# Wide column copies in the opening of a fused network, and a line-innermost spectrum with inner statistics in its third layer

## Chip, cores and metric

One NeuronCore of a Trainium2 chip runs the whole network in one launch, in float32. The metric is the device time of one execution in microseconds (us); lower is better. Engines are named as in the profile: PE (TensorE matmuls), PEld (TensorE's loads of stationary weights, which overlap PE), DVE (VectorE), ACT (ScalarE), POOL (GpSimd), SP (SyncE, which issues all DMAs here). SBUF and PSUM are the two on-chip memories, of 128 partitions each; matmuls write PSUM.

## The reference

Four images of 64x64 pixels with 128 channels pass four layers. Each adds to its input: `x = x + layer(group_norm(x))`.

- Layer 0 is a selective scan. A projection makes 256 channels and 256 gates per pixel; the channels go through a 3x3 depthwise convolution and a SiLU. The result is scanned along four paths: by rows, by columns, and both backwards. Per path a projection gives step sizes `delta`, `B` and `C`, and with 16 states a channel `h = exp(delta*A)*h + delta*u*B` runs over all 4096 pixels, `y = h*C`. The sum is normed, multiplied by SiLU of the gates, projected.
- Layer 1 multiplies low Fourier modes along each axis and applies two dense layers.
- Layer 2, the third, treats each of the 128 channels of an image as a token, a 64x64 picture ("CoDANO"). Instance norm `in(.)` is over the pixels of one token:

```python
tn   = in1(tokens)
k, q, v = (spectral_conv(tn, w) + skip for w in (key, query, value))   # 16 heads; k, q at 32x32
attn = softmax(q k^T / scale) v
attn = in_a(spectral_conv(attn, proj_w) + skip + tokens)               # spectral_conv: rfft2, low modes x w, irfft2
m    = in2(attn)
m    = gelu(in_m1(spectral_conv(m, mixer_w1)) + skip1(m))
m    = in_m2(spectral_conv(m, mixer_w2)) + skip2(m)
out  = in_o(m) + attn
```

- Layer 3 is attention in 7x7 neighbourhoods.

## The kernel before

**Layer 0.** An image is `[channels, pixels]`, in two halves `s` of 128 channels and eight chunks `c` of 512 pixels (eight rows of the image). The scan takes, for 128 units (image, path, chunk) of 16 states each, POOL's product `dB` (L651), ACT's `dA` (L656) and DVE's scan (L657); `units[0]` is chunk 0 by rows, unit 8 the first by columns. Everything else of this layer runs beside the scans from a table of slots, except for the **opening** (`opening`, from L190), which must come before the first scan and has its own written order.

The opening reads image 0, norms it (L215 to L217), and then for `c` = 0 to 5 (`DENSE = 6`): `scale` norms the chunk and projects half 1 (L224 to L227); `padded` copies half 0's chunk with its border (POOL, L234); `depthwise` convolves half 1 on DVE, nine operations (L241, L248); `conv` convolves half 0 on PE in nine passes (L164); `gates` makes the two gates. `silu` is three ACT passes and a product on DVE, with a DMA of the result: `e = exp(-v)`, `ln(1+e)`, `exp(-e)` (L198 to L200), `e = v*e` (L343). `grown` ends a convolved half with its `silu` and with `by_columns` (L351 to L355): ACT copies the chunk into a tile `xw` with columns outermost, and an SP DMA writes it to DRAM array `xw0`, where a column's 64 pixels lie together; a chunk has eight rows, so each run is 8 floats, 32 B. The gates of chunks 6 and 7 follow. `e`, `xw` and other tiles share four buffers (tag `t2`). Into the list `steps` are woven the inputs of unit 0: after chunk 1 `fetch` (u), after chunk 3 `begun` (projection `xd_ps`, copies `xc` and `cc`, and `Bb`, the broadcast of B from DRAM, of three buffers), after chunk 4 `readied` (`d`, `e`, `l`, `m` of both halves: projection `dp`, exp, log, limit; then `du` on POOL). For these and `dp` a bank of PSUM comes from `spare` (one bank, tag `m`).

**Layer 2.** `layer2_image` (L1070 on) is a generator that issues one image's instructions and yields at each wait. `Pace.in_turn` advances two images at a time, always the one whose modelled time is least; `Pace.spend` keeps the modelled time of engines (all of the layer's instructions are recorded at its line, L1043, in the profile). The order that it finds is fixed at build time. The stages are: load and group norm; `token_stats` of the input (`bn_stats` of 32 blocks of 128x128, then three small products `in_pm`); `dft_y`, a transform along lines (PE, to PSUM `pu`, ACT copies it to `U`); `px`, the second transform (PE loads a slice of `U` as weights); `pv`, `pG`, a Gram matrix for the attention scores; scores, softmax `S`; `pk` for the skips; `pz`, the attention-weighted product for both images of the pair (weights `WX`); `synthesis` (PE `pa`, ACT copy to `S2`, PE `pb`; its `put` adds `pb` to `z`); the statistics of `z`, from which the norm's scale `sa` and shift `za`; then twice `spectral` (`dft_y`, `pq` times `mix`, `synthesis`, whose `put` copies to `sp`), with statistics of `sp` behind each; mixing with `m` and gelu behind the first; and the tail behind the second: `sp` scaled and added to `m`, statistics of `m`, `x` loaded again into `sp`, and `z*sa + f3 + m*q3 + x` to the output. `by_rows` is one DVE operation on 128x1024 with a scale for each token; `affine` is eight ACT operations on 128x128. Images 0 and 1 run together, then 2 and 3.

In `U`, of shape `[P, 64, 2, 32]`, the transformed axis is innermost, so the slice for one frequency, over 64 lines, steps by 64 floats:

```python
nc.tensor.matmul(px[:, e, :], lhsT=U[:, :, q, 4 * g + e], rhs=w["quad"][:, q, :], ...)
```

and in `V`, `[66, 64, 8]`, the slice `V[:, :, e]` steps by 8 floats.

Of the kernel before, what the change touches and what calls it, by code (L numbers as in the profile page):

```python
# [84 lines left out]
def layer0(sh, A, x_in, x_out, scr):  # L85
# [7 lines left out]
    with ExitStack() as ctx:  # L93
# [79 lines left out]
        def grown(b, c, s, pm, later, e=None):  # L173
            bias = conv_b[:, s : s + 1], conv_nb[:, s : s + 1]
            xo = silu(pm, *bias, scr(f"xr{b % 2}")[s, :, c * CH : (c + 1) * CH], later, (0, 1, 2), e)
            later("act0", by_columns, xo, scr(f"xw{b % 2}")[s], c, slots=4)

        def gates(b, c, v, bank, later):
            for s in range(2):
# [3 lines left out]
                silu(zp, 0.0, 0.0, scr(f"z{b % 3}")[s, :, c * CH : (c + 1) * CH], later, (0, 0, 1))  # L183
# [6 lines left out]
        def opening(bank, steps):  # L190
# [3 lines left out]
            def soon(place, f, *a, slots=1, **kw):  # L194
                if place == "dve" or f is by_columns:
                    waiting[place[:3]].append(lambda: f(*a, **kw))
                else:
                    f(*a, **kw)  # L198

            now = lambda place, f, *a, slots=1, **kw: f(*a, **kw)  # L200
            pair = lambda name: tmp.tile([P, 2, CH], F32, name=name, tag="t4", bufs=4)
# [52 lines left out]
            for c in range(DENSE + 1):  # L254
# [6 lines left out]
                if last:  # L261
                    grown(0, c - 1, 0, last[0], soon, pair("e")[:, 0])
                    grown(0, c - 1, 1, last[1][:, 0], soon, last[1][:, 1])
# [14 lines left out]
            for c in range(DENSE, NCH):  # L278
                for _ in gates(0, c, xg[:, 8 * c : 8 * c + 8], bank, now):
# [135 lines left out]
        def inputs(k, c, u, par):  # L415
# [64 lines left out]
        def fetched():  # L480
            u, v = fetch(*units[0])
            do, ready, bd, Wd = inputs(*units[0][1:], v, 0)
# [6 lines left out]

        def readied():  # L490
            for name in ("d0", "e0", "l0", "m0", "d1", "e1", "l1", "m1", "du"):
# [119 lines left out]
        with tc.manual_schedule(engines=order):  # L611
            idle = lambda: None
            left = opening(any_bank, [idle, fetched, idle, begun, readied])
            u, ready, bd, Wd, Bb = (got[n] for n in ("u", "ready", "bd", "Wd", "Bb"))
            sides.append(Side(rest(left, spare, later), 18 * len(left), 0, 2 * NS * len(left)))
            for i, (b, k, c) in enumerate(units):
# [22 lines left out]
                for n in range(NS):  # L639
# [34 lines left out]
                    if i + 1 < len(units):  # L674
                        if n == 1:
                            u_next, v_next = fetch(*units[i + 1])
                            do, ready_next, bd_next, Wd_next = inputs(*units[i + 1][1:], v_next, (i + 1) % 2)
# [335 lines left out]
class Pace:  # L1013


    def __init__(self, nc):
        self.nc, self.free, self.t, self.first = nc, {}, 0.0, None

    def spend(self, name, op, out):
# [11 lines left out]
        self.free[name] = end  # L1031
        self.first = self.first or name
# [45 lines left out]
def layer2_image(sh, w, pools, x_in, x_out, scr, wt, parity, beside):  # L1078
# [16 lines left out]
    def token_stats(src):  # L1095


        st = own([P, NJ, 6], "in_st")
        for j in range(NJ):
            nc.vector.bn_stats(st[:, j, :], src[:, j, :])  # L1100
            if j % 8 == 7:
                yield j == NJ - 1
# [44 lines left out]
    def dft_y(src):  # L1147

        U = large("U2", [P, 64, 2, 32])
        for g in range(NJ // 4):  # L1150
# [3 lines left out]
            nc.scalar.copy(U[:, 8 * g : 8 * g + 8].rearrange("p t q r -> p (t q r)"), pu.rearrange("p q m -> p (q m)"))  # L1154
# [3 lines left out]
    def synthesis(Z, put):  # L1158
# [20 lines left out]
        for g0 in range(0, 16, 4):  # L1179
# [13 lines left out]
            yield g0 == 12  # L1193

# [68 lines left out]
    for g in range(8):  # L1263
        px = ps.tile([64, 4, Q], F32, name="px", tag="b")
        for e in range(4):
            for q in range(2):
                nc.tensor.matmul(
                    px[:, e, :], lhsT=U[:, :, q, 4 * g + e], rhs=w["quad"][:, q, :], start=(q == 0), stop=(q == 1)
# [25 lines left out]
    for v, r0, r1 in ((1, 0, 8), (2, 8, 9), (0, 9, 16), (3, 16, 17), (0, 17, 24), (1, 24, 32), (None, 0, 0)):  # L1294
        nr = r1 - r0
        if nr:
            V = tmp.tile([66, 64, 8], F32, name="V2", tag="S2", bufs=3)
            pv = ps.tile([66, 64, nr], F32, name="pv", tag="a")
            for q in range(2):
                nc.tensor.matmul(pv, lhsT=w["gram"][:, v, q, :], rhs=U[:, :, q, r0:r1], start=(q == 0), stop=(q == 1))  # L1300
            nc.scalar.copy(V[:, :, :nr], pv)
        if V_last is not None:
            for e in range(V_last[1]):
                Ve = V_last[0][:, :, e]
# [135 lines left out]
    yield from synthesis(Zp, lambda u, g0, p: tt(at(z, u, g0), at(z, u, g0), p, ALU.add))  # L1440
# [3 lines left out]
    mu, var = yield from token_stats(z)  # L1444
# [17 lines left out]
    def spectral(src, mix):  # L1462
        U = yield from dft_y(src)
        Zm = own([Q, 64, 32], "Zp", tmp)
        for g in range(4):
            px = ps.tile([Q, 16, 32], F32, name="pq", tag="b")
            for q in range(2):
                nc.tensor.matmul(
                    px, lhsT=w["quad"][:, q, :], rhs=U[:, 16 * g : 16 * g + 16, q, :], start=(q == 0), stop=(q == 1)
                )  # L1470
            tt(Zm[:, 16 * g : 16 * g + 16, :], px, mix.unsqueeze(1).to_broadcast([Q, 16, 32]), ALU.mult)
# [532 lines left out]
```

## Time and profile before

| quantity | value |
|---|---|
| time before, median of 3 runs | 7942.88 us (7941.58 to 7944.81) |
| the profiled execution's own time | 7939.57 us |
| its span, first to last instruction | 7937.7 us |
| mean granted TensorE clock | 0.959 |

Stretches of the profiled execution, busy us of each engine:

| stretch (us from the span's start) | length | PE | DVE | ACT | POOL |
|---|---|---|---|---|---|
| opening, to the first scan: 0 to 153.2 | 153.2 | 86.9 | 85.8 | 78.6 | 19.3 |
| scans of layer 0: to 5790 | 5636.8 | 4595.8 | 5388.4 | 5189.6 | 5175.6 |
| layer 1: to 6319 | 529.0 | 454.5 | 298.0 | 150.8 | 0.0 |
| layer 2: to 7366 | 1047.0 | 760.9 | 565.0 | 340.3 | 102.0 |
| layer 3: to 7937 | 571.0 | 493.8 | 430.8 | 386.0 | 191.3 |

In the lines that follow, a group of instructions reads: line, engine, operation, output and input by the program's names, shapes, count | busy us, mean ns of one | idle time of the engine just before them and what ended it. A line of a timeline reads: start, duration, engine, line, operation, and in brackets the wait before it with what ended it. A line of the chain of waits reads: start, length, engine, tile, line, number of instructions. A line by stretches reads: the stretch, its length, then PE, PEld, DVE, ACT and POOL busy with counts, granted clock, DMA share and GB/s.

### The profile page before, as it was taken

The numbers are of one execution on the slowest core, as the hardware profiler recorded it, in microseconds if no ns is written. First come the engines' busy times: TensorE is split into PE (matmuls) and PEld (weight loads), VectorE is DVE, ScalarE is ACT, GpSimd is POOL, SyncE is SP. The second block draws the span as 40 slices with busy tenths as digits, with TensorE's granted clock in tenths as the row PEclk, the third lists the DMA queues.
The fourth block names the chain that finished last, engine by engine and source line by source line (L and its number), as shares of the span: only waits on it lengthen the run. The fifth ranks groups of instructions, "written<-read, shape, count | busy, mean of one in ns | idle before, by whom it ended". The sixth has DMA issues, their size and how long they took to land. (4 is left out here: it accounts for less than half of the span.)

```text
span 7937.7 us, 140991 instructions
## 1 busy us (share of the span) xinstructions
PE 6391.9 (81%) x52796; PEld 4053.1 (51%) x52796; DVE 6768.0 (85%) x8012; ACT 6145.3 (77%) x9814; POOL 5488.2 (69%) x2510
## 2 busy tenths in 40 slices
PE   6888888878888877888987777787778888686789
PEld 2544444444455444445554444454457665464566
DVE  6999999999999999999999999999845645645678
ACT  5999999999999999999999999999822223315567
POOL 2989999988999998999999999999800010020233
PEclk8999999999999999999999999999989988788899
DMA  9556556545556554555555445555442230331332
GB/s 149 161 169 176 176 173 176 168 165 167 188 172 185 179 169 165 172 183 177 177 187 169 167 162 182 175 172 188 149 111 46 55 106 21 91 106 39 99 95 80
DMA packets 1392574, 1159.91 MB, mean 146 GB/s; under 512 B 759829, under 2 KB 1186417, under 8 KB 1324946
## 3 DMA queue, kind: packets, MB, share of 16 engines
q1 hardware_dynamic: 1390210, 1149.16, 47.9%
q8 instruction: 416, 6.82, 0.4%
q14 instruction: 268, 2.20, 0.1%
q10 hardware_dynamic: 1680, 1.74, 0.1%
HBM read 956.89 MB, written 189.74 MB: 144 GB/s over the span
## 5 line engine op out<-in xcount | busy, mean ns | idle before, releaser
L657 DVE TENSOR_TENSOR_SCAN h<-dA,state,dB 128x512 f32<-128x512 f32 x4096 | 4920.2, 1266 | 191.6 <-ACT dA L656 71.3
L651 POOL TENSOR_TENSOR dB<-du,Bb 128x1024 f32<-128x1024 f32 x2048 | 4812.5, 2388 | 358.8 <-DVE h L657 237.6
L511 PE MATMUL pt<-ident,h 128*128 128x128 f32 x16384 | 2219.5, 279 | 872.2 <-ACT hT L521 861.2
L656 ACT ACTIVATE dA<-delta,A_neg 128x512 f32<-128x512 f32 x4096 | 2760.5, 697 | 151.7 <-DVE h L657 123.8
L511 PEld LDWEIGHTS pt<-ident,h 128*128 128x128 f32 x16384 | 1809.5, 141 | 1923.0 <-ACT hT L521 1706.2
L521 ACT COPY hT<-pt 128x1024 f32<-128x1024 f32 x2048 | 2079.6, 1015 | 164.0 <-PE pt L511 144.9
L546 PE MATMUL yT<-hT,W 128*32 128x256 f32 x16384 | 1378.0, 409 | 1.0 <-ACT hT L521 0.6
L1043 POOL COPY XG<-Xs 64x9 f32<-64x9 f32 (+2 forms) x44 | 10.9, 292 | 960.5 <-ACT Xs L1043 960.5
L546 PEld LDWEIGHTS yT<-hT,W 128*32 128x32 f32 x16384 | 454.9, 150 | 339.9 <-issue 327.4
L164 PE MATMUL cv<-xn,taps 128*128 128x512 f32 x936 | 526.9, 644 | 2.8 <-DVE delta L451 2.8
L1724 POOL TENSOR_TENSOR S<-S,sm 128x784 f32<-128x784 f32 x128 | 191.3, 1494 | 436.4 <-DVE sm L1722 366.7
L454 POOL TENSOR_TENSOR du<-delta,u 128x1024 f32<-128x1024 f32 x128 | 304.7, 2381 | 96.9 <-DVE delta L451 96.9
L442 PE MATMUL dp<-xd,w_dt 65*128 65x512 f32 x512 | 289.9, 648 | 68.8 <-ACT Ct L433 41.3
L425 PE MATMUL xd_ps<-u,w_x 128*48 128x512 f32 x512 | 248.9, 609 | 44.9 <-DVE e L343 39.4
L1731 ACT ACTIVATE S<-S,mx 128x196 f32<-128x196 f32 x512 | 227.9, 448 | 35.2 <-DVE mx L1758 34.6
L164 PEld LDWEIGHTS cv<-xn,taps 128*128 128x128 f32 x936 | 139.2, 188 | 180.7 <-issue 160.6
L851 ACT ACTIVATE h<-pf,b 128x512 f32<-128x512 f32 x128 | 88.0, 687 | 145.0 <-PE pf L850 145.0
L451 DVE SCALAR_TENSOR_TENSOR delta<-delta,dp 128x512 f32<-128x512 f32 x256 | 170.7, 667 | 13.9 <-ACT delta L448 10.7
L1686 PE MATMUL pt<-ident,S 128*98 128x128 f32 x1024 | 167.0, 288 | 3.6 <-POOL S L1724 1.9
L448 ACT ACTIVATE delta<-delta 128x512 f32<-128x512 f32 x256 | 165.9, 648 | 0.1
L442 PEld LDWEIGHTS dp<-xd,w_dt 65*128 65x128 f32 x512 | 76.6, 188 | 173.9 <-ACT Ct L433 94.4
L445 ACT ACTIVATE delta<-dp 128x512 f32<-128x512 f32 x256 | 153.0, 598 | 9.8 <-PE dp L442 8.4
(366 smaller groups left out, 6934.2 us busy)
## 6 DMA issues: line engine op xcount, KB each, us to landing
Bb<-l_B SPq DMA_DIRECT2D x512, 1024.0 KB
W<-l_W SPq DMA_DIRECT2D x512, 256.0 KB
l_y<-y SPq DMA_DIRECT2D x128, 512.0 KB
u<-l_xr SPq DMA_DIRECT2D x64, 512.0 KB
u<-l_xw SPq DMA_DIRECT2D x64, 512.0 KB
y<-l_y SPq DMA_DIRECT2D x56, 512.0 KB
V<-l_v SPq DMA_DIRECT2D x512, 49.0 KB
y<-l_y SPq DMA_DIRECT2D x80, 256.0 KB
```

The costliest lines, as they stand in the source:

```text
L164: nc.tensor.matmul(pm, lhsT=taps[:, s, t, :], rhs=xn[:, dy : dy + 8, dx : dx + 64], start=(t == 0), stop=(t == 8),)
L425: nc.tensor.matmul(bank["x"], lhsT=w_x[:, s, k, :], rhs=u[:, s, :], start=(s == 0), stop=(s == 1))
L442: nc.tensor.matmul(bank[s], lhsT=w_dt[:, k, s * P : (s + 1) * P], rhs=xd, start=True, stop=True)
L454: nc.gpsimd.tensor_tensor(du, delta, u, ALU.mult)
L511: nc.tensor.transpose(pt[:, j, s, :], G["h"][:, s, t0 : t0 + 32, :].rearrange("p t n -> p (t n)"), sh.ident)
L521: return lambda: nc.scalar.copy(hT, pt.rearrange("p j s d -> p j (s d)"))
L546: nc.tensor.matmul(U["yT"][e][32 * jo : 32 * jo + 32, qo % 2, :], lhsT=U["Ws"][G["g"]][:, :, 4 * q + j], rhs=hT[:, j, :], start=((e, jo) n ...
L651: nc.gpsimd.tensor_tensor(dB, du, B_now[:, q : q + 1, :].to_broadcast([P, 2, CH]), ALU.mult)
L656: nc.scalar.activation(dA, delta[:, s, :], AF.Exp, scale=A_neg[:, k, s, n : n + 1])
L657: nc.vector.tensor_tensor_scan(h[:, s, :, q], dA, dB[:, s, :], state[:, s, n : n + 1], ALU.mult, ALU.add)
L1724: nc.gpsimd.tensor_tensor(Sv, Sv, U["sm"].unsqueeze(2).to_broadcast([P, 4, 196]), ALU.mult)
L1731: nc.scalar.activation(Sn, Sn, AF.Exp, bias=U["mx"][:, n : n + 1], accum_out=sm[:, n : n + 1])
```

## The change

Opening:

- `gather` takes the place of `by_columns`. ACT copies each chunk into a wide tile for four chunks (`[P, 4, 512]`, from the three buffers of `Bb`), columns outermost, so that a column of the tile has 32 rows; one DMA for each half writes chunks 0 to 3 after chunk 3's copy (runs of 128 B, 1 MB), and one for each half chunks 4 and 5 after chunk 5's (runs of 64 B, 512 KB).
- The gates of chunks 6 and 7 get buffers of their own (`pair("e")`, tag `t4`).
- `readied` is split: `d`, `e`, `l` of both halves in chunk 4's turn, `m` and `du` in chunk 5's; their order is d0, d1, e0, e1, l0, l1. The opening takes their banks from `any_bank`, four in turn.

Layer 2:

- `U` becomes `[P, 2, 32, 64]`, `V` `[66, 8, 64]`, `pq` `[Q, 32, 16]`: lines innermost. The weights of `px` and both operands of `pG` are then read without a step. ACT's copy into `U` reads PSUM with a step of 64 floats and DVE's product of `pq` reads it with a step of 16 floats.
- The statistics of `z` and of both `sp` are taken inside `synthesis`, four blocks behind each `put` (`counted`). `Pace` charges them to DVE without advancing the image's own time (`aside`).
- `residual`: POOL replaces `z` by `z*sa + za + x` in place, three operations on 128x1024 for each of four quarters, issued during the first `spectral`; `x` is loaded there, into a buffer of its own, `xr`.
- `grown`: POOL scales `m` by the second skip's weight during the second `spectral` (four operations on 128x1024).
- Tail: 32 DVE operations on 128x128 make `m = sp*q2 + m`, each eight followed by their statistics. Then, for three quarters, `affine` on ACT (`m*q3 + f3`) and one addition of `z` on DVE; for the last, eight DVE operations `m*q3 + z` and one `by_rows` with `f3`.

```diff
-            later("act0", by_columns, xo, scr(f"xw{b % 2}")[s], c, slots=4)
+            later("act0", gather or by_columns, xo, scr(f"xw{b % 2}")[s], c, slots=4)
...
+            def gather(xo, s, c):
+                n = 4 if c < 4 else DENSE - 4
+                first = c % 4 == 0
+                if first:
+                    wide[s] = tmp.tile([P, 4, CH], F32, name="xw", tag="Bb", bufs=3).rearrange("p q t -> p (q t)")
+                t = wide[s][:, : 512 * n].rearrange("p (w h) -> p h w", w=64)
+                h0 = 8 * (c % 4)
+                nc.scalar.copy(t[:, h0 : h0 + 8], xo.rearrange("p (h w) -> p h w", w=64))
+                if c % 4 == n - 1:
+                    nc.sync.dma_start(
+                        scr("xw0")[s].rearrange("p (w h) -> p w h", h=64)[:, :, 8 * c - 8 * n + 8 : 8 * c + 8],
+                        t.rearrange("p h w -> p w h"),
+                    )
...
-                for _ in gates(0, c, xg[:, 8 * c : 8 * c + 8], bank, now):
+                es = pair("e")
+                for _ in gates(0, c, xg[:, 8 * c : 8 * c + 8], bank, now, (es[:, 0], es[:, 1])):
...
+        def grown_steps():
+            for name in ("d0", "d1", "e0", "e1", "l0", "l1"):
+                got["do"][name]()
+
         def readied():
-            for name in ("d0", "e0", "l0", "m0", "d1", "e1", "l1", "m1", "du"):
+            for name in ("m0", "m1", "du"):
                 got["do"][name]()
...
-            left = opening(any_bank, [idle, fetched, idle, begun, readied])
+            left = opening(any_bank, [idle, fetched, idle, begun, grown_steps, readied])
...
+    def counted(st, src, js):
+        nc.aside = True
+        for j in js:
             nc.vector.bn_stats(st[:, j, :], src[:, j, :])
+        nc.aside = False
...
-        U = large("U2", [P, 64, 2, 32])
+        U = large("U2", [P, 2, 32, 64])
...
-            nc.scalar.copy(U[:, 8 * g : 8 * g + 8].rearrange("p t q r -> p (t q r)"), pu.rearrange("p q m -> p (q m)"))
+            nc.scalar.copy(
+                U.rearrange("p q r t -> p (q r) t")[:, :, 8 * g : 8 * g + 8],
+                pu.rearrange("p j m -> p (j m)").rearrange("p (t k) -> p k t", t=8),
+            )
...
-                    px[:, e, :], lhsT=U[:, :, q, 4 * g + e], rhs=w["quad"][:, q, :], start=(q == 0), stop=(q == 1)
+                    px[:, e, :], lhsT=U[:, q, 4 * g + e, :], rhs=w["quad"][:, q, :], start=(q == 0), stop=(q == 1)
...
-                Ve = V_last[0][:, :, e]
+                Ve = V_last[0][:, e, :]
                 nc.tensor.matmul(pG, lhsT=Ve, rhs=Ve, start=(n_done == 0), stop=(n_done == 31))
...
-    yield from synthesis(Zp, lambda u, g0, p: tt(at(z, u, g0), at(z, u, g0), p, ALU.add))
+    st = own([P, NJ, 6], "in_st")
+
+    def added(u, g0, p):
+        tt(at(z, u, g0), at(z, u, g0), p, ALU.add)
+        counted(st, z, block(u, g0))
+
+    yield from synthesis(Zp, added)
...
+        def copied(u, g0, p):
+            nc.scalar.copy(at(sp, u, g0), p)
+            counted(st, sp, block(u, g0))
+            nc.aside = True
+            next(beside, None)
+            nc.aside = False
...
+    def residual():
+        xr = large("xr")
+        load_image(nc, xr, x_in)
+        for n, c in enumerate(C4):
+            wide = lambda v: v[:, c].unsqueeze(2).to_broadcast([P, 8, DM])
+            for v, op in ((wide(sa), ALU.mult), (wide(za), ALU.add), (xr[:, c, :], ALU.add)):
+                nc.gpsimd.tensor_tensor(z[:, c, :], z[:, c, :], v, op)
+            if n % 2:
+                yield
...
+    def grown():
+        for n, c in enumerate(C4):
+            nc.gpsimd.tensor_scalar(m[:, c, :], m[:, c, :], scal(10), None, ALU.mult)
+            yield
...
-        if n % 2:
-            by_rows(sp, sp, q2, n, ALU.mult)
-        else:
-            affine(sp, sp, q2, None, n)
-        stt(m[:, c, :], m[:, c, :], scal(10), sp[:, c, :], ALU.mult, ALU.add)
-        nc.sync.dma_start(sp[:, c, :], x_in[1024 * n : 1024 * n + 1024, :].rearrange("(j p) d -> p j d", p=P))
+        js = range(8 * n, 8 * n + 8)
+        for j in js:
+            stt(m[:, j, :], sp[:, j, :], q2[:, j : j + 1], m[:, j, :], ALU.mult, ALU.add)
+        counted(st, m, js)
...
-        affine(z, z, sa, f3, n)
-        by_rows(m, m, q3, n, ALU.mult)
-        tt(m[:, c, :], m[:, c, :], sp[:, c, :], ALU.add)
-        yield False
-        tt(m[:, c, :], m[:, c, :], z[:, c, :], ALU.add)
+        if n == 3:
+            for j in range(8 * n, 8 * n + 8):
+                stt(m[:, j, :], m[:, j, :], q3[:, j : j + 1], z[:, j, :], ALU.mult, ALU.add)
+            by_rows(m, m, f3, n, ALU.add)
+        else:
+            affine(m, m, q3, f3, n)
+            yield False
+            tt(m[:, c, :], m[:, c, :], z[:, c, :], ALU.add)
```

## The prediction

> **What bounds the kernel now.** I read the page first, then the timeline of the opening by queue, the groups by shape in the third layer's stretch, its chain of waits and its busy time by stretch. The page says that no engine bounds the whole:
>
> ```profile
> PE 6391.9 (81%) x52796; PEld 4053.1 (51%) x52796; DVE 6768.0 (85%) x8012; ACT 6145.3 (77%) x9814; POOL 5488.2 (69%) x2510
> ```
>
> DVE's 85% is the first layer's scan (4920.2 us), which the change leaves alone. It touches two stretches: 0 to 153.2 us, before the first scan, and the third layer, from its first load at 6319 to 7366. In the opening, ACT's timeline shows who holds the first scan back:
>
> ```profile
> 131.65 0.60 ACT L200 ACTIVATE e<-zp 128x512 f32<-128x512 f32 x1 [4.39 <-DMA l_xw<-xw]
> 137.31 0.60 ACT L200 ACTIVATE e<-zp 128x512 f32<-128x512 f32 x1 [3.74 <-DMA l_xw<-xw]
> 143.96 0.60 ACT L200 ACTIVATE e<-zp 128x512 f32<-128x512 f32 x1 [4.74 <-DMA l_xw<-xw]
> 150.60 0.60 ACT L200 ACTIVATE e<-zp 128x512 f32<-128x512 f32 x1 [4.72 <-DMA l_xw<-xw]
> 153.20 20.22 DVE L657 TENSOR_TENSOR_SCAN h<-dA,state,dB 128x512 f32<-128x512 f32 x17
> ```
>
> Gates 6.3 us apart, each waiting for the tile of a column copy: a 256 KB column copy of 8192 runs of 32 B costs the DMA engines 6.3 us, and twelve of them stand in this stretch.
>
> In the third layer the weight loads of two groups stand out, beside one that reads its weights without a step:
>
> ```profile
> L1043 PEld LDWEIGHTS pz<-PT,WX 128*68 128x68 f32 x2048 | 131.8, 146 | 20.0 <-DVE WX L1043 17.1 <-POOL WX L1043 1.7 <-issue 1.1
> L1043 PEld LDWEIGHTS px<-quad,U 128*64 128x64 f32 x512 | 57.8, 204 | 2.1 <-ACT U L1043 1.7
> L1043 PEld LDWEIGHTS pG<-V 66*64 66x64 f32 x256 | 32.5, 216 | 10.7 <-issue 10.3 <-ACT V L1043 0.3
> ```
>
> Busy by count: pz 64 ns a pass, px 113, pG 127. The chain has them at 112.7 (px x96 in 10.82), 126 (pG x30 in 3.79), 62.4 (pz x544 in 33.94).
>
> Then its back half, where the chain goes through statistics while PE stands:
>
> ```profile
> 7118.65 6.40 PE pb L1043 x24
> ...
> 7125.77 10.84 DVE in_st L1043 x56
> ...
> 7136.66 5.33 PE in_pm L1043 x24
> ...
> 7335.29 6.20 DVE in_st L1043 x32
> ```
>
> ```profile
> 7320.00:7370.00 50.00, 2.95 (x12) 2.71 (x12) 35.00 (x62) 21.33 (x60) 0.00 (x0) 0.50 0.42 122
> ```
>
> In the last 50 us PE works 2.95, DVE 35, ACT 21, POOL nothing: elementwise work.
>
> **Opening.** Twelve column copies become four: two of 8192 runs of 128 B (1 MB), two of 8192 runs of 64 B. Undisturbed, a chunk takes 10.44 us (L227's copies at 40.58 and 51.02: ACT's silus 8, DVE's product and scale 1.2, PE's pv 1.1). So L227 of chunk 3 comes at 61.5 instead of 65.7; chunk 4 at 74.1 (PE: conv to 70.9, xd_ps 1.9, pv 0.9); chunk 5 at 87.1 (two dp, two exp, two ln, which now run side by side). The column copies of chunk 4 follow at 95.1. They take a buffer from the three of "Bb", and the first two wide DMAs must have left it: issued at 84.5. Their price: by the descriptor count 6.3 us each, by bytes (256 KB in 6.3) 25 us each. I take 8: the count is unchanged, the runs are longer. They land at 92.5 and 100.5, so ACT stands 4.5 us. Then silus of chunk 5 (3.9), two copies (1.9), four gates on own buffers (4x1.81): first scan at 115.5. Queued behind SP's two 64 B transfers are now the second and third Bb, which wait for that landing: Bb lands near 125, where the fifth row of scans wants its product; I charge 3. Gain 153.2-115.5-3 = 35 (28 to 42). A column copy into a step of 128 B has no row; the one with a step of 32 B takes 1.13 us, one without a step 0.59; I keep 1.13 (0.6 to 2.2, twelve of them, a chunk's worth hidden by PE's 10.3 us). The gates' own buffers and the three banks for the first dp and xd_ps have no instruction; their worth is in the sum.
>
> **Front of the third layer.** px's weights and both operands of pG lose their step. px mirrors pz then (64 columns loaded, 68 streamed): 64 ns. 512x(113-64) = 25, 256x(126-64) = 16, together 41. Up to 7100 the chain holds 7.2% + 3.9% of 784 us, 87 of their 95.5 busy: 37 us gained. Both ends: 0, if the loads are slow for another reason, and 41.
>
> Here a rule stands against the change. ACT now copies U out of PSUM with a step of 256 B, and DVE multiplies pq with a step of 64 B:
>
> ```profile
> L1043 ACT COPY Zp<-pz 68x512 f32<-68x512 f32 x16 | 9.3, 582 | 140.9 <-PE pz L1043 140.9
> ```
>
> This copy already reads with that very step and takes 582 ns, the plain U copy 585. The Trainium skill ("SBUF — State Buffer", Door 1: The DMA port swizzle, its note on cachelines) gives PSUM lines of 8 B and SBUF lines of 16 B and a penalty for each access that leaves its line. For SBUF weights row and rule agree. For PSUM the row denies it on ACT: 96 U copies cost nothing more; doubled they would add 0.55 at each of 12 tails, 7 us. For DVE no row reads PSUM with a step: 0.69 as now, or 1.02 as TENSOR_REDUCE Pb with a step beside 0.69 for mx; PE's 1.72 per pq hides all but eight tails, 0 to 3 us, I take 1, inside the rounding.
>
> **Back half, by pairs of images.** Statistics of z are taken block by block beside PE's 1.9 us per pair of pb: of 10.84 us 0.8 remains, -10. Statistics of sp likewise; the second image's (4x1.55) leave the first's mixing, so the second mixes 14 us sooner. What is added: per image twelve POOL operations on z (128x1024), put from the first step of the first synthesis on. By dB (2.38 us) 24 take 57 us a pair, by Z<-TT,W alone 1.90. Whom they meet:
>
> ```profile
> 6458.51 1.90 POOL L1043 TENSOR_TENSOR Z<-TT,W 128x1024 f32<-128x1024 f32 x1 [20.06 <-DVE TT L1043]
> ...
> 6459.05 1.51 DVE L1043 SCALAR_TENSOR_TENSOR BI<-BD,tok_cols,ident 128x128 f32<-128x128 f32 x1
> ...
> 6487.06 0.35 DVE L1043 SCALAR_TENSOR_TENSOR BI<-BD,tok_cols,ident 128x128 f32<-128x128 f32 x1
> ```
>
> The same operation takes 0.35 alone and 1.51, to POOL's end, beside it. The skill (same page, Who interferes with whom) says why: a DVE instruction with two SBUF inputs and a POOL instruction that reads SBUF exclude each other for a whole instruction, one with a single SBUF input does not. Statistics and everything from PSUM are free, then; norms have four two-input operations each, mixing eight an image. Without the rule this costs 0; if each waits, four small ones 7 us before the first image's mixing and three or four large ones another 7: 14, which I take. So the mixing stage gains about nothing net. Behind it a new wait: in the changed order ACT's first copy into U of mix2 waits for POOL, since the tile takes the buffer of the residual; POOL ends about when the last gelu does, each us later counts whole.
>
> Tail: DVE had per image statistics 6.2+6.2, four stt 5.1, two by_rows 2.4, twelve tt 14.7: 34.6. It gets 40 stt of 128x128 (0.35 alone with its drain; statistics of that size follow at 0.194; I take 0.26): 10.4, 6.2 statistics, four 128x1024 operations 4.9: 21.5. Per pair 69 to 43, plus 6 us of the second image's statistics, for which the first's stt now wait in DVE's queue: 20; less 3 for POOL's scaling of m (no row; a copy of 128x640 takes 0.91, so 1.5, at most 2.38): 17. ACT's 32 z and 16 sp scalings give way to 24 of m an image, beside DVE. The residual loads go earlier on SP, where DMA is idle (share 0.00 from 6600 to 6760).
>
> Second pair: 10+0+17 = 27, with a late start of pa 26. First pair 20: its tail (6827 to 6850) lies beside the next images' statistics. 46 in all (15 to 70).
>
> **Sum.** 35+37+46 = 118. Against the profiled execution, 7939.57 (span 7937.7 and 1.9 around it): 7821.6. The median of the runs is 3.3 above it, so 7825.
>
> **Rivals.** (1) Column copies cost by bytes: 25 us for each wide one, landing at 134; the first scan near 151, opening gain 2, 7858. For it: all else in the queue runs by bytes; against: the copies moved 256 KB in 6.3 us while Bb moves 1 MB in about as long. (2) Weight loads don't speed up: 7862. Against: both slow groups have a step, pz and psc (165 ns a load) have none. (3) Slower: the port. With my charges for it undone (2x14 for the residual, 2x3 for the scaling of m) the gains are 152. If all 48 residual operations and the 16 scalings of m stop DVE's chain for 2.69 us each (the mean of the twelve Z<-TT,W of before, 32.3 us, most of them contended), that is 172: 20 us slower, 7963. It decides above 152/64 = 2.4 us of DVE's chain for each POOL operation; against it, statistics and reads of PSUM go on beside POOL, and the chain rests on PE and ACT for part of the stage. (4) The port costs little and tails shrink by all that DVE loses: 70 in the back, 40 in the opening: 7796.
>
> **Chances.** Forecast 0.60; (1) 0.10, (2) 0.10, (4) 0.16, (3) 0.04. What a measurement of this kernel can tell from no change is about 0.2%, 16 us. Slower 0.03 (from (3)), same 0.02 (the rest of (3), and (1) and (2) together), faster 0.95. The range reaches from (4) with the best of the bounds to (2): 7788 to 7868.
>
> **What would show it.** First scan at 110 to 120 and no ACT wait for l_xw above 6 us (right); at 140 or more, (1). px and pG loads of 60 to 70 ns a pass; above 100, (2). in_st between pb and in_pm under 2 us. DVE two-input operations of 2 to 3 us in the mixing, beside POOL's residual; U of mix2 waiting for POOL by more than 5 us would make me wrong in the mixing stage. The forecast is wrong if the third layer does not come below 990 us (1047 now) or the opening below 128.

## The result, and the profile after

| quantity | before | after |
|---|---|---|
| median of 4 runs, us | 7942.23 (7939.49 to 7944.81) | 7841.72 (7829.51 to 7852.11) |
| the profiled execution's own time, us | 7939.57 | 7839.47 |
| its span, us | 7937.7 | 7837.7 |
| mean granted TensorE clock | 0.959 | 0.962 |

The change makes the kernel faster by 100.5 us: the ratio of after to before is 0.9873 [0.9856, 0.989]. The prediction had 118 us, so some 17 are missing.

By engine, the page after:

```profile
PE 6346.8 (81%) x52796; PEld 4010.0 (51%) x52796; DVE 6755.1 (86%) x8112; ACT 6108.1 (78%) x9714; POOL 5634.8 (72%) x2574
```

PE works 45 us less than before and ACT 37, POOL 147 us more, and the span is 100 us shorter. So the change took out work of PE and ACT as well as waits, and moved some of it to POOL. To place the gain I read times at the same events of both timelines. "Opening" is the start of the first scan. Layer 2 runs its images in two pairs, and each pair is cut at the first `pu` of its input, the first `pz`, the first `pa` behind it, the first `pu` of `z`, the first `pu` of `m`, and the end (the next pair's first `pu`, or DVE's last operation on `m`).

| stretch, us (layer 2: pair 1, pair 2) | before | after | difference |
|---|---|---|---|
| opening | 153.2 | 111.8 | -41.4 |
| front | 132.1, 133.4 | 118.8, 127.8 | -13.3, -5.6 |
| `pz` | 76.8, 75.3 | 76.3, 75.5 | -0.5, +0.2 |
| synthesis of `z`, its statistics and norm | 47.8, 47.8 | 39.2, 38.4 | -8.6, -9.4 |
| first `spectral` and mixing | 83.7, 84.2 | 77.0, 78.5 | -6.7, -5.7 |
| rest: second `spectral`, tail | 177.6, 136.5 | 170.3, 129.5 | -7.3, -7.0 |

Layer 2 gives 63.9 in the profiled executions. The opening's 41.4 has shrunk to 31.3 by the last scan (which starts at 5743.2 before and 5711.9 after). The other 4.9 of the 100.1 lie in layer 3, which the change leaves alone: over the fourteen profiles of this study its length lies between 567.3 and 575.2 us without a pattern, and the profile of before has the longest.

**The opening.** ACT's timeline after:

```profile
93.92 1.07 ACT L210 COPY xw<-e 128x512 f32<-128x512 f32 x1
96.78 1.08 ACT L210 COPY xw<-acc 128x512 f32<-128x512 f32 x1 [1.79 <-DMA l_xw<-xw]
...
103.80 0.61 ACT L200 ACTIVATE e<-zp 128x512 f32<-128x512 f32 x1
...
105.64 0.58 ACT L200 ACTIVATE e<-zp 128x512 f32<-128x512 f32 x1
```

Before, each of these gates waited 3.7 to 4.7 us for a column copy's tile. Now the four follow each other every 1.81 us (two are shown), and what is left is a wait of 1.79 for a column copy. The scans begin, on DVE, and POOL makes their products:

```profile
111.84 9.51 DVE L679 TENSOR_TENSOR_SCAN h<-dA,state,dB 128x512 f32<-128x512 f32 x8
125.57 3.63 DVE L679 TENSOR_TENSOR_SCAN h<-dA,state,dB 128x512 f32<-128x512 f32 x3 [4.23 <-POOL dB L673]
```

```profile
123.20 6.96 POOL L673 TENSOR_TENSOR dB<-du,Bb 128x1024 f32<-128x1024 f32 x3 [6.40 <-DMA Bb<-l_B]
```

After eight scans DVE stands for 4.23 us, because POOL waited 6.40 for `Bb`. This is the wait for which the prediction charged 3.

**The front.** Groups of the third layer after, by shape:

```profile
L1067 PEld LDWEIGHTS px<-quad,U 128*64 128x64 f32 x512 | 33.8, 146 | 2.2 <-ACT U L1067 1.7
L1067 PEld LDWEIGHTS pG<-V 66*64 66x64 f32 x256 | 16.6, 138 | 10.8 <-issue 9.8 <-ACT V L1067 0.3
L1067 ACT COPY U<-pu 128x512 f32<-128x512 f32 x96 | 55.7, 585 | 78.1 <-PE pu L1067 77.9
L1067 DVE TENSOR_TENSOR Zp<-pq,mix 68x512 f32<-68x512 f32 x32 | 21.7, 682 | 43.8 <-PE pq L1067 43.8
```

The 512 passes of `px` load their weights in 33.8 us, 66 ns each instead of 113; the 256 of `pG` in 16.6, 65 ns instead of 127. The copy into `U`, which now reads PSUM with a step, takes 585 ns as before, and the product of `pq`, which reads it with a step too, 682 ns (685 before).

**The back half.** The chain of waits after, at the end of the synthesis of `z`, in the mixing, and in the tail of the second pair:

```profile
7055.88 0.88 DVE in_st L1067 x4
7056.80 2.83 PE in_pm L1067 x16
...
7118.01 1.57 DVE in_d L1067
...
7126.27 1.98 DVE in_d L1067
...
7128.55 1.52 DVE q L1067
...
7130.54 1.55 DVE f L1067
```

```profile
7253.44 9.35 ACT m L1067 x24
...
7262.81 3.34 DVE m L1067 x9
```

Where 10.84 us of statistics stood ahead of `in_pm`, 0.88 stands now. In the mixing four tiny DVE operations of the norms take 1.5 to 2.0 us each, beside POOL's residual. And the tail's end begins with ACT's 24 affines, 9.35 us.

### The profile page after: what moved, and what is told of

Same layout as the page of the kernel before. It is cut to its first block, busy times and chain, and to the rows that moved or that the text cites. A ratio compares the mean times of both kernels' runs of the same rounds, so it can differ in the third digit from the quotient of the medians.

```text
span 7837.7 us, 141040 instructions
## 1 busy us (share of the span) xinstructions
PE 6346.8 (81%) x52796; PEld 4010.0 (51%) x52796; DVE 6755.1 (86%) x8112; ACT 6108.1 (78%) x9714; POOL 5634.8 (72%) x2574
## 5 line engine op out<-in xcount | busy, mean ns | idle before, releaser
L1067 POOL TENSOR_TENSOR WX<-wr,Xs 128x544 f32<-128x544 f32 x40 | 57.3, 1434 | 148.4 <-issue 62.1
```

What stands on the lines that cost most here:

```text
L1067: r = f(*args, **kw)
```

## Experiments

Times are medians. Each ratio is to the kernel before in runs on the same chip, with its 95% interval. The changed kernel's own ratio is 0.9873 [0.9856, 0.9890]; it, e1 to e4, e5 to e8 and e9 to e12 ran at different times, the last three groups on three chips, so times of two such groups are compared only roughly.

| run | time, us | ratio |
|---|---|---|
| e1: opening alone | 7907.25 | 0.9962 [0.9947, 0.9977] |
| e2: layout alone | 7915.86 | 0.9974 [0.9965, 0.9983] |
| e3: inner statistics alone | 7916.79 | 0.9973 [0.9964, 0.9982] |
| e4: `residual`, `grown` and tail alone | 7951.17 | 1.0013 [1.0005, 1.0021] |
| e5: e4 with `m`'s statistics charged | 7938.71 | 0.9999 [0.9991, 1.0008] |
| e6: changed, narrow column copies | 7853.40 | 0.9890 [0.9875, 0.9904] |
| e7: changed, two POOL operations a quarter | 7834.09 | 0.9864 [0.9849, 0.9878] |
| e8: changed, matmuls that keep PE busy | 7852.09 | 0.9889 [0.9875, 0.9904] |
| e9: changed, again | 7838.56 | 0.9876 [0.9859, 0.9892] |
| e10: changed, `Bb` issued early | 7832.78 | 0.9869 [0.9854, 0.9884] |
| e11: changed, own buffers for POOL's products | 7840.21 | 0.9879 [0.9864, 0.9894] |
| e12: changed, with e7, e10 and e11 | 7827.47 | 0.9863 [0.9848, 0.9877] |

Layer 2 by stage, cut as above, from one profiled execution of each (pair 1, pair 2). A kernel that leaves a stage alone repeats it within about 2 us, so smaller differences are not read. The exception is the second pair's front with the new layout, which lies between 123.7 and 127.8 us in eight kernels; the changed kernel's is the longest.

| run | front | synthesis of `z` | mixing | rest |
|---|---|---|---|---|
| before | 132.1, 133.4 | 47.8, 47.8 | 83.7, 84.2 | 177.6, 136.5 |
| e2 | 119.5, 126.4 | 47.8, 47.8 | 83.7, 84.0 | 177.6, 136.8 |
| e3 | 133.5, 134.9 | 39.2, 39.2 | 72.7, 72.7 | 186.2, 144.8 |
| e4 | 131.7, 133.6 | 47.8, 47.8 | 89.4, 89.0 | 175.2, 138.3 |
| e5 | 132.3, 133.3 | 47.8, 47.8 | 89.9, 88.8 | 172.3, 129.8 |
| after | 118.8, 127.8 | 39.2, 38.4 | 77.0, 78.5 | 170.3, 129.5 |

### One part at a time: e1 to e4

```diff
 e1: before, with the opening's hunks of the change
 e2: before, with the hunks of U, V and pq
 e3: before, with the statistics inside synthesis, for z and both sp:
+    counted(st, z, block(u, g0))     # in z's put
+    counted(st, sp, block(u, g0))    # in sp's put
 e4: before, with residual, grown and the new tail; statistics of z and sp stay behind their synthesis
```

> The kernel before with the opening's part of the change alone. Theory: the parts are independent in time, and the opening keeps what the two traces show (first scan 41.4 us earlier, 37.5 left after the first unit, 35 after the eighth, 31.3 at the last scan): 31 to 37 us faster, third layer 1047 as before. Rival: the stages do not add (the whole gained 100 because of what the third layer's order does with an earlier start): under 25 us.

> The kernel before with the line-innermost U, V and pq alone. My prediction put 37 us on it. Theory from the traces: PE saves 20.6 us of passes in each pair of images, but the first pair's front keeps 13 and the second's about 5, because PE then stands for the second image's statistics or the products Z and runs slower after standing: 17 to 24 us faster, px and pG loads near 66 ns a pass. Rival: it was the altered order of the whole change that spoilt the second front, and alone the layout gives 33 to 40 us.

> The kernel before with the statistics of z and sp inside the synthesis alone. Theory (as predicted): 10 us at the statistics of z in each pair and 6 to 14 at those of sp in the mixing: 25 to 40 us faster. Rival: what the statistics of sp give is lost again, since the mixing of both images then stands in one row on ACT and DVE: 16 to 22 us, that of z alone.

> The kernel before with POOL's residual, POOL's scaling of m and the new tail alone. Theory: 10 to 11 us less in each tail, as the second pair's tail shows in the two traces, less what POOL's operations take from DVE (about 7 us in the mixing of each pair): 10 to 22 us faster. Rival: without the earlier statistics POOL's operations meet only statistics and the lock costs nothing: 25 us or more.

Against before (7938.95 on the same chip) e1 moved the run by -31.7 us, e2 by -23.1, e3 by -22.2 and e4 by +12.2. That is -65 in all, and the whole is -100: the parts depend on each other. The stage table says where. Front, synthesis and mixing add up: in the mixing e3 gives -11.0 and -11.5, e4 costs 5.7 and 4.8, and the whole shows -6.7 and -5.7. The rest does not add up: e3 is worse there by 8.6 and 8.3, e4 differs little (-2.4, +1.8), and the whole is better by 7.3 and 7.0.

What e3 loses there is to be seen in the last 50 us of layer 2 to DVE's end, before, in e3 and then in the changed kernel:

```profile
7312.50:7362.60 50.10, 5.93 (x24) 5.42 (x24) 42.03 (x76) 23.82 (x66) 0.00 (x0) 0.50 0.39 115
```

```profile
7295.80:7345.90 50.10, 5.93 (x24) 5.42 (x24) 45.28 (x97) 25.30 (x66) 0.00 (x0) 0.50 0.37 105
```

```profile
7217.40:7267.40 50.00, 8.27 (x36) 7.90 (x36) 38.93 (x137) 19.54 (x51) 0.80 (x4) 0.51 0.36 102
```

In e3 DVE is busy for 45.28 of 50.1 us, 42.03 before (the 35.00 that the prediction read is of a window that ends 7.5 us behind DVE's last operation). ACT's scalings of `z` and `sp` had 16.5% of the chain of waits in this stretch before and have nothing of it in e3. So I read it thus: with its statistics done earlier each image comes sooner to the old tail, whose DVE work now stands nearly in one row and sets the end. e3 gives back at the end three quarters of what it gains in the mixing. The new tail leaves DVE 38.93 of 50.0.

e4's loss in the rest of the second pair has another cause, which PE's timeline shows:

```profile
7302.89 1.99 PE L1045 MATMUL pb<-S,bd 64*128 64x512 f32 x8
7311.77 1.06 PE L1045 MATMUL in_pm<-in_st,tok 128*128 128x32 f32 x4 [6.89 <-DVE in_st L1045]
...
7313.50 3.76 PE L1045 MATMUL pa<-sy,Zp 68*128 68x256 f32 x8
```

PE stood for 6.89 us at `in_pm`, for the statistics of one image's `m`, with `pa` and `pb` of the other image behind it in the queue; and when it went on, eight passes of `pa` took 3.76 us instead of some 1.9. `Pace` had put them in this order because `aside` leaves the image's modelled time where it was before its statistics.

### The order in the tail: e5

```diff
     def counted(st, src, js):                             # against e4
-        nc.aside = True
         for j in js:
             nc.vector.bn_stats(st[:, j, :], src[:, j, :])
-        nc.aside = False
+            nc.free["vector"] += 0.13
+            nc.t = nc.free["vector"] + 0.1
```

> The tail alone again (as in the run before it was 12 us slower), but with the statistics of m charged in the planner's account at their true cost, so that the products of one image's statistics stand behind the other image's pa and pb in PE's queue. Theory: the loss was one of order, PE standing 9.7 us before a pa behind in_pm, in both pairs: it comes back by 8 to 20 us, to 7930 to 7945. Rival: the loss is POOL's lock on DVE, which this leaves as it is: 7948 to 7955.

Now the other image's `pa` and `pb` stand ahead of `in_pm`:

```profile
7297.57 1.99 PE L1045 MATMUL pa<-sy,Zp 68*128 68x256 f32 x8
7299.50 1.99 PE L1045 MATMUL pb<-S,bd 64*128 64x512 f32 x8
7304.52 0.89 PE L1045 MATMUL in_pm<-in_st,tok 128*128 128x32 f32 x4 [3.03 <-DVE in_st L1045]
```

The rest is 2.9 and 8.5 us shorter than in e4, and the run 12.5 us. (The two ran on different chips; each against the kernel before on its own chip, the difference is 17 us, and the intervals of their ratios overlap from 1.0005 to 1.0008 only.) In this order the tail alone neither gains nor loses: its -5.3 and -6.7 in the rest stand against +6.2 and +4.6 in the mixing. So of the 36 us by which the whole is better than the sum of its parts, 12 to 17 are a matter of e4's order, which the whole doesn't share. With e5 for e4 the stage table still misses 10.6 and 8.9 us in the rest. These I put down to the new tail taking away the DVE work that held e3 back; e3's chain speaks for it and its 45.28 only weakly, and no run has the inner statistics and the new tail alone together, so it is argued and not shown.

### Gates' buffers or wide copies: e6

```diff
-    grown(0, c - 1, 0, last[0], soon, pair("e")[:, 0], gathers[0])
+    grown(0, c - 1, 0, last[0], soon, pair("e")[:, 0])     # by_columns, as before; half 1 likewise
```

> The changed kernel with the opening's twelve narrow column copies put back, and the gates' own buffers, the four banks and the split of readied kept. Theory: the narrow copies' 6.3 us each are most of the opening's gain, though gates in own buffers no longer wait for them, so the first scan comes at 125 to 140 and the kernel is 10 to 25 us slower than with wide copies: 7850 to 7868. Rival: the gates' waits were all of it (they are what ACT's timeline of before shows), and the wide copies give nothing: first scan by 116, 7838 to 7846.

The first scan came at 131.0 us, the run at 7853.40, 11.7 us above the changed kernel (their ratios overlap; the first scan's 19 us are clear). ACT's timeline of e6 has waits of the old kind again, but none of the gates waits:

```profile
93.71 1.12 ACT L372 COPY xw<-acc 128x512 f32<-128x512 f32 x1 [3.80 <-DMA l_xw<-xw]
...
115.35 1.12 ACT L372 COPY xw<-acc 128x512 f32<-128x512 f32 x1 [4.77 <-DMA l_xw<-xw]
```

So of the 41 us ahead of the first scan the gates' own buffers, the banks and the split of `readied` give 22, the wide copies 19.

### POOL's share in the mixing: e7

```diff
-    for v, op in ((wide(sa), ALU.mult), (wide(za), ALU.add), (xr[:, c, :], ALU.add)):
+    for v, op in ((wide(sa), ALU.mult), (xr[:, c, :], ALU.add)):
...
+    tt(f3, f3, za, ALU.add)       # 128x32, ahead of the tail's affines
```

> The changed kernel with two POOL operations in place of three for each quarter of the residual: za goes into the shift f3 of the tail. The output is the same. Theory: POOL is done some 15 us sooner in each pair, before the second image's norm in the mixing, whose small DVE operations of 1.4 to 2.0 us (0.2 alone) then run at 0.2: about 5 to 7 us a pair, 10 to 14 in all. Rival: these operations are not on the path (ACT's gelus and affines are): 0 to 4 us.

The run came at 7834.09, 7.6 us below the changed kernel and 4.5 below its repeat e9, with overlapping ratios. The mixing is clearer: 74.1 us in both pairs, 3 to 4 less than in the changed kernel. The norms on DVE in the second pair, in the changed kernel and then in e7:

```profile
7126.27 1.98 DVE L1067 TENSOR_TENSOR in_d<-in_d 128x64 f32<-128x64 f32 x1
...
7128.55 1.51 DVE L1067 TENSOR_SCALAR q<-q,scal 128x32 f32<-128x32 f32 x1
```

```profile
7124.20 0.22 DVE L1067 TENSOR_TENSOR in_d<-in_d 128x64 f32<-128x64 f32 x1
...
7124.72 0.24 DVE L1067 TENSOR_SCALAR q<-q,scal 128x32 f32<-128x32 f32 x1
```

The same operations take about 0.2 us where POOL has ended: at 7117.1 in e7, at 7134.5 in the changed kernel. The one of e7 that still meets POOL (`in_d` at 7115.26) takes 1.96. This is the exclusion that the prediction weighed from `BI` and the Trainium skill ("SBUF — State Buffer", Who interferes with whom), and the runs agree with it for `in_d`, which reads two tiles. `q<-q,scal` reads one.

### Keeping PE busy: e8

```diff
+    def keep_busy(out, n):        # shortened: matmuls whose result the next product overwrites
+        for _ in range(n):
+            matmul(out, lhsT=w["tok"], rhs=w["tok"][:, : out.shape[1]], start=True, stop=True)
...
+    keep_busy(pm[:, 0, :], 20)    # 32 columns, ahead of in_pm of the input
...
+    keep_busy(psc[:, 0, :], 20)   # 64 columns, ahead of psc
```

> The changed kernel with 20 matmuls of no use (their output is overwritten) in PE's queue ahead of the statistics' products of the input and ahead of the scores' product psc, where PE stands for about 3 us. Theory: the front lost half of the layout's gain because PE, standing for 3 us, is granted half its clock for the next 10 us; kept busy it keeps its clock, px and pu behind in_pm run at 70 and 125 ns a pass, and each pair gains 3 to 7 us: 6 to 14 us faster than the changed kernel. Rival: the clock falls for another reason (or the filling delays as much as it saves): within 4 us, or slower.

This asks what became of the front's gain. PE's timeline in the second pair's front, before and then after:

```profile
6896.09 9.11 PE L1043 MATMUL px<-quad,U 128*64 128x68 f32 x80 [0.68 <-ACT U L1043]
6905.13 0.64 PE L1043 MATMUL in_pm<-in_st,tok 128*128 128x32 f32 x4
...
6908.63 3.76 PE L1043 MATMUL px<-quad,U 128*64 128x68 f32 x32
...
6957.52 3.15 PE L1043 MATMUL psc<-TT,Z 128*64 128x64 f32 x96
```

```profile
6827.90 4.95 PE L1067 MATMUL px<-quad,U 128*64 128x68 f32 x80 [0.68 <-ACT U L1067]
6836.02 1.06 PE L1067 MATMUL in_pm<-in_st,tok 128*128 128x32 f32 x4 [3.17 <-DVE in_st L1067]
...
6840.86 3.89 PE L1067 MATMUL px<-quad,U 128*64 128x68 f32 x32
...
6883.68 4.53 PE L1067 MATMUL psc<-TT,Z 128*64 128x64 f32 x92 [3.79 <-DVE Z L1067]
```

The first 80 passes of `px` take 4.95 us instead of 9.11. But then PE stands 3.17 us for DVE's statistics of the second image, which it did not before, and what follows is slow: 32 passes of `px` take 3.89, as long as the 3.76 with the slow loads. The stretch behind that wait shows a halved clock, before and then after (the number ahead of the DMA share is the granted clock):

```profile
6905.00:6913.50 8.50, 8.10 (x68) 7.73 (x67) 2.05 (x11) 2.10 (x5) 0.53 (x3) 1.00 0.15 33
```

```profile
6836.00:6846.40 10.40, 10.02 (x66) 9.56 (x67) 2.03 (x10) 1.62 (x4) 1.07 (x8) 0.50 0.00 0
```

At `psc` PE waits 3.79 us for `Z`, and 92 passes take 4.53 where 96 took 3.15.

The fillers brought nothing: the run's median is 10 us above the changed kernel's (the ratios overlap), the fronts are 125.9 and 127.4, the rest 176.1 and 129.7. By stretches of e8:

```profile
6820.70:6829.00 8.30, 8.30 (x42) 8.30 (x40) 4.06 (x14) 0.00 (x0) 0.00 (x0) 0.50 0.00 0
6907.60:6910.70 3.10, 3.10 (x98) 3.03 (x97) 0.02 (x1) 0.00 (x0) 0.61 (x5) 1.00 0.03 5
6854.70:6859.20 4.50, 4.50 (x43) 4.45 (x40) 3.23 (x17) 0.48 (x1) 0.00 (x0) 1.00 0.30 66
6862.80:6868.40 5.60, 5.24 (x39) 4.98 (x39) 1.56 (x8) 1.14 (x3) 1.08 (x8) 0.50 0.00 0
```

Behind the fillers of 64 columns `psc` ran at full clock, in 3.1 us: the pause is what halves it there. With the fillers of 32 columns it is otherwise. One set (from 6820.7) came when the clock was at half already, 6.6 us after a stop of PE of 8.22 us; it kept PE busy for 8.3 of 8.3 us, and the clock stayed at 0.50. Another (from 6854.7) filled the place of the 3.17 us pause at full clock, without a gap, and yet the clock was at 0.50 from 6862.8 on. The Trainium skill ("TensorE: Matmul & The Clock Gate", Part 1: The HAM clock gate (the "warmup" mystery)) makes half rate the default, released by some 3.4 us of sustained activity and back after an idle window of that length. The falls after pauses of 3.17 and 3.79 us are near that. The 8.3 us of small matmuls without a release and the fall without a pause do not agree with it, nor do the 10.02 busy us of 10.40 at 0.50 in the changed kernel, so a full queue alone is not what is measured. What is, these runs don't show. Each set of fillers took 4.6 to 8.6 us in line with PE's other work.

### A repeat and three repairs: e9 to e12

```diff
 e9: the changed kernel
 e10: chunks 4 and 5 are gathered in pair("xw") instead of a buffer of Bb's, and in readied:
+    got["Bb1"] = broadcast(got["bd"], 1)     # the first unit takes it as its second Bb
 e11:
-    Zn, zt = Z[:, n], Z[:, 3]
+    Zn, zt = Z[:, n], Z[:, (3, 2, 3)[n]]
 e12: the edits of e7, e10 and e11 together
```

> The changed kernel itself once more, on the same chip as the three that follow: 7830 to 7850.

> The changed kernel with the second broadcast of B issued ahead of the column copies of chunks 4 and 5, and those copies in other buffers (tag t4). Theory: the 4 us that the scan stands at its fifth row (POOL waiting 6.4 us for Bb, which was queued behind these copies and the gates' stores) go, and nothing else: first scan as before the edit (111 to 113), kernel 3 to 6 us faster than the changed kernel. Rival: the broadcast only changes places with the column copies, whose late landing holds up ACT and the gates: first scan later by 4 us or more, no gain.

> The changed kernel with POOL's products for Z in two buffers by turns, so that POOL needn't wait for DVE's sum before the next. The order of all queues is the same. Theory: half of what the front of the third layer gave back is psc waiting for Z (3.5 to 4.9 us in each image of a pair, and psc at half clock after it); the three products then stand in a row on POOL, Z is ready some 2 to 4 us sooner, 1 to 2 waits a pair on the path: 4 to 10 us faster than the changed kernel, fronts of 113 to 117 and 121 to 126 us (118.8 and 127.8 now). Rival: POOL and DVE exclude each other in these operations anyway, so Z comes no sooner: within 2 us.

> The last two edits and the two POOL operations of e7 together: 12 to 22 us faster than the changed kernel, 7818 to 7830, if they add.

e9 took 7838.56 us (7836.91 to 7840.96) beside the other three.

In e10 the second `Bb` is issued at 95.77 us; in the changed kernel it stood behind the column copies and the gates' stores until 116.53. DVE's first scans then stand in one piece:

```profile
113.56 16.56 DVE L685 TENSOR_TENSOR_SCAN h<-dA,state,dB 128x512 f32<-128x512 f32 x14
```

The first scan starts 2 us later, and the stall of 4.23 is gone. The median is 5.8 us below e9's, but the runs overlap (7823.63 to 7841.68), so the size is not settled; 2.7 us of it may be the second front (123.7 against 126.4 in e9), with which the edit has nothing to do. There half clock ended 6.8 us after the 3.17 us pause, where in the changed kernel it lasts some 13.5.

In e11 POOL's two products for `Z` have buffers of their own. In the first pair, after and then e11:

```profile
6380.42 2.93 POOL L1067 TENSOR_TENSOR Z<-TT,W 128x1024 f32<-128x1024 f32 x1 [20.40 <-DVE TT L1067]
...
6383.38 1.23 DVE L1067 TENSOR_TENSOR Z<-Z 128x1024 f32<-128x1024 f32 x1 [1.80 <-POOL Z L1067]
```

```profile
6383.66 4.79 POOL L1067 TENSOR_TENSOR Z<-TT,W 128x1024 f32<-128x1024 f32 x2 [20.40 <-DVE TT L1067]
...
6386.62 2.91 DVE L1067 TENSOR_TENSOR Z<-Z 128x1024 f32<-128x1024 f32 x1 [1.80 <-POOL Z L1067]
```

POOL's products run in a row, but DVE's `Z<-Z` now meets the second of them and takes 2.91 us instead of 1.23: the exclusion again. The fronts (119.1 and 126.3; 119.0 and 126.4 in e9) and the run (7840.21) gain nothing.

e12 took 7827.47 us (7824.05 to 7831.92), 11.1 below e9 without overlap, and a little less than expected. It is the fastest kernel of the study.

## Why the prediction was right, and where it was wrong

**Opening: predicted -35, came as -31.7 (e1).** The first scan came at 111.8, not 115.5. The wide copies were cheaper than the 8 us each that were taken: the DMA records have the 16384 runs of 128 B of both between 84.0 and 95.9 us, 6.0 us a copy, which is the price by count; rival (1), a price by bytes, would be 50 us for the two. ACT's copies into the wide step took 1.05 to 1.12, as taken. The term that was mis-sized is the 3 for `Bb` queued behind them: 4.2 were lost at once, and 10 by the last scan. Stores of the units show 37.5 us kept after the first unit and 35 after the eighth; where the rest goes, over 5 ms in which the start of the last scan varies by 4 to 6 us between executions with one opening, was not tried.

**Front: predicted -37, came as -19.** This is the step that failed: "the chain holds 7.2% + 3.9% of 784 us, 87 of their 95.5 busy: 37 us gained". The loads did become as fast as claimed, 40 us in all, so rival (2) falls. The step on PSUM costs nothing on ACT (585 ns) or DVE (682), so the row was right. The note on cachelines in the Trainium skill ("SBUF — State Buffer", Door 1: The DMA port swizzle) is borne out by the loads, which read SBUF; for PSUM it speaks of slower matmuls, and the penalty that the prediction read from it for ACT and DVE did not come. But the chain's share of an operation says how long it stood on the path, not how much it can shrink until something else stands there. The two fronts before and then after, pair 1 and pair 2 each (length, then PE's busy time first):

```profile
6367.17:6499.31 132.14, 115.86 (x833) 90.35 (x834) 48.76 (x96) 36.49 (x65) 23.75 (x29) 0.88 0.34 84
6885.35:7018.71 133.36, 115.72 (x834) 90.66 (x835) 53.44 (x100) 36.50 (x65) 23.83 (x29) 0.88 0.36 91
```

```profile
6336.07:6454.86 118.79, 94.97 (x833) 70.04 (x834) 48.76 (x96) 36.22 (x65) 23.74 (x29) 0.85 0.37 94
6817.73:6945.57 127.84, 102.13 (x833) 75.97 (x834) 53.35 (x100) 36.23 (x65) 23.81 (x29) 0.80 0.38 95
```

In pair 1 PE works 20.9 us less, but stands 7.5 us more (23.8 instead of 16.3): the whole loss is waits. In pair 2 it stands 8.1 us more (25.7 instead of 17.6) and works only 13.6 us less, 7.3 short of pair 1, at a granted clock of 0.80 against 0.85. So of some 42 us (twice the 20.9) about 16 went to new waits and 7 to PE running slower, which I put down to the clock. DVE's statistics and the products of `Z` were hidden just behind the loads, and they came forth as waits of 3.17 and 3.79 us in pair 2 and of 4.61 at `psc` in pair 1. e2 alone shows the same fronts (-12.6, -7.0), so it is not the altered order of other parts.

**Statistics of `z`: predicted -10, came as -8.6 and -9.4.** Right, by the step itself: 0.88 us in the chain instead of 10.84.

**Mixing: predicted about 0 (-14 for an earlier second image, +14 for the port), came as -6.7 and -5.7.** Both terms were too large: e3 gives -11, and `residual` costs about 5 (e4). Their errors, 3 and 9 us, undo each other in part. Of the port's two sevens the small operations' was right: five of them lost 1.2 to 1.8 us each, 7 in all. Statistics went on beside POOL as taken, eight in 1.64 us. But "one with a single SBUF input does not" leaves out a condition: the page ("SBUF — State Buffer", Who interferes with whom) says it of DVE instructions outside the two-port modes, and names `tensor_scalar` among those that can enter them. `q<-q,scal` is one, and it was held up (1.51 us against 0.24); its mode no run here shows. The large ones' was wrong: POOL had ended (7134.5) when the sums of `m` began (7135.3). The new wait that was named, ACT's first copy into `U` of the second `spectral` behind POOL, did not come, since that copy started 20 us later (7154.8), behind ACT's own affines and gelus. Rival (3) needed 2.4 us of DVE's chain for each POOL operation; 5 us for the 24 of a pair is 0.2.

**Tail: predicted -17 in the second pair, came as -7.0.** DVE's sum was right where it can be read: eight small operations take 2.17 to 2.19 us, 0.27 each against 0.26 taken. Mis-sized was what ACT does meanwhile: "24 of m an image, beside DVE". For the last image they are ahead of DVE, not beside it. From the start of the affines to DVE's end it is 14.0 us (7253.4 to 7267.4), and ACT's 9.35 of them hold DVE back: it stands for 3.31, 1.85 and 1.85 us ahead of its three sums, 7.0 of the 10 that are missing. The rest is not placed.

**Back half in all: predicted -46, came as -44.7** (pair 1 -22.6 for 20, pair 2 -22.1 for 26). The total is right by luck, with the mixing 6 too small in each pair and the second pair's tail 10 too large: a sum that fits does not prove its terms. It was also added up as if each part brought its share by itself, which e3 and e4 deny.

**Sum.** The profiled executions differ by 100.1: 31.3 in the opening and the scans, 18.9 in the fronts, 44.7 in the back half, 0.3 at `pz`, 4.9 in layer 3. Against 118 the fronts are 18 short, the opening 4 and the back half 1, and layer 3's 5 are no part of the change.

## What to carry to other kernels

The share of the chain that an operation holds bounds a gain from above: before it is counted in full, look a few us behind it for the next engine's work: here that took 16 of 42 us. New pauses of PE of 3 to 4 us had half clock behind them as well, but filling them with small matmuls (e8) cost more than it gave. Work taken off an engine pays only where that engine sets the end, so two parts that meet in one stage may each give little alone and more together, and are tried together before one is dropped. Work put on POOL stopped small DVE operations, of two tiles and one of one tile, until POOL's instruction ended; fewer POOL instructions on the path's stretch (e7) help where closing POOL's gaps (e11) does not.

## What the hardware showed that was not expected

POOL's scaling of `m` by a column of scalars takes longer than a POOL product or sum of two operands of that size. The prediction took 1.5 us and at most 2.38; the sixteen take 2.84 to 3.26, off the path:

```profile
7121.88 1.89 POOL L1067 TENSOR_TENSOR z<-z,sa 128x1024 f32<-128x1024 f32 x1
...
7189.81 2.85 POOL L1067 TENSOR_SCALAR m<-m,scal 128x1024 f32<-128x1024 f32 x1 [6.64 <-ACT sp L1067]
```

A DVE `TENSOR_SCALAR` of one 128x32 tile by a column of scalars (`q<-q,scal`) was held up to the end of POOL's instruction at 7130.0, while the `RECIPROCAL` of the same tile just before it took 0.34 us as it does alone. And matmuls of 32 columns, without a gap for 8.3 us, left the granted clock at 0.50, and behind another set of them it fell to 0.50 without a pause (e8).
